# MLP gates of a decoder layer: the side pass's subtractions moved to VectorE at three fixed places, signs stored in the base's tile, VectorE and TensorE in written order

## The chip, the cores and the metric

One core of a Trainium2 chip runs the whole kernel in one launch. The time is the device time of that core in microseconds (us). The core's engines run side by side, each in its own instruction order: TensorE (PE, with PEld for its weight loads), VectorE (DVE), ScalarE (ACT), GpSimd (POOL) and SyncE (SP, which here only issues DMAs). They meet through semaphores. TensorE writes its products to eight banks of PSUM; everything else lies in SBUF.

## The reference

A decoder layer in float32 on 2 x 512 tokens of width 1024: a Mamba-2 block with a gated MLP behind it, a product with a quantized context, and a gated FFN whose weights are rebuilt from a base and the signs of a difference. What matters here are the MLP and what the FFN needs of its weights:

```python
h2 = rmsnorm(h, ln2_w)
mlp = silu(h2 @ gate_w.T) * (h2 @ up_w.T) @ down_w.T      # INTER = 3584
...
def _binary_diff_weight(w, base):
    d = w - base
    coeff = jnp.mean(jnp.abs(d))
    return base + coeff * jnp.sign(d)
W1 = _binary_diff_weight(w1, mean_w1)
W2 = _binary_diff_weight(w2, mean_w2)
W3 = _binary_diff_weight(w3, mean_w3)
```

The mean of |d| runs over a whole weight matrix, so the kernel must have passed over all of w1, w2 and w3 before the FFN begins. It does this pass beside the MLP: it stores the signs in bf16 and sums the absolute values.

## The kernel before

**Stages.** The MLP ("m") and the FFN ("f") use the same two functions: `gates` makes silu(gate) * up and stores it with the differences of the down weights, `down` multiplies them. `gates` takes the 3584 columns in 14 groups of 256 (NG, GW). A group is one 2 x 2 block product by Winograd's form of Strassen's scheme with seven block products; two of the seven pairs are split once more by `second_level`. So a group has, on TensorE, `second_level` "m" (products 1 and 2 of the outer scheme, L779, tiles mm{i}a to d), `second_level` "n" (6 and 7, tiles mn{i}a to d) and three calls of `one` (products 5, 4 and 3, L857, tiles m{i}c and m{i}d). Groups 0 and 1 have plain products in place of "m" (`first_two`, L328, tile ma).

**Banks.** "m" and the calls of `one` use four of the eight banks (X), "n" the other four (Y); the next group has them the other way round. In `second_level` bank b is written by product 6, read by VectorE's add u2, and written again by product 7; bank c is written by product 5, read by the add c22, and written on by product 3. Bank a is copied to p1 by ScalarE (L786) ahead of u2. Inside one, the written order on TensorE is a1, b6, c5, d4, b7, a2, c3.

**VectorE's work of a group** (helpers `add` L187 and `sub` L190): five adds that empty the banks in each `second_level`; the add to O12 (mo, 128x1024); two adds of 128x1024 that end in `turn` (L888); two adds each for the banks of products 5 and 4 (the last add of product 4 gives block 21) and two for product 3 (`finished`); `left`, the block differences of the next group's gate and up weights (four each, tiles mg{i}s and mu{i}s, and four more for "n"); `outer_left`, four more for "m" (tile my and others); `down_blocks`, four for the down weights; four products of silu(gate) and up (L925, tile mh); `hidden_blocks`, four differences of mh. `left`, `outer_left` and `down_blocks` may not be issued ahead of `turn`. Apart from that the scheduler orders VectorE and TensorE: it puts what is ready first, earlier lines ahead of later ones. In group 1 there are four more of 128x1024 (`second_level_right`, B12).

**The deferred part.** In the MLP a group's last steps wait in the list `late` and are written inside the next group: `finished` (the two adds for product 3, Silu, the product of slot 3) behind the copy of bank a, `put` (`hidden_blocks` and the store of mh) behind the "m" `second_level`.

**The side pass** (`Diffs`, only in the MLP, 34 steps, three a group, the last in group 11). A step takes one group of w1, w3 or w2 (128x2048 float32, 1 MB, and as much for the base). GpSimd loads both by its own DMA queue (tiles sw with two buffers and smean_w with one, L1137), subtracts (L1152) and stores the signs (L1142); ScalarE computes Sign into a bf16 tile sg (L1161) and Abs with a running sum (L1162). ScalarE's order in this stage is the written one (`on_act`, a chain of `issue_after` edges, which fix an order on one engine without a wait); GpSimd's is too (`on_pool`). `Diffs.step` is called in the "n" `second_level` (`between`), after the three first products of silu and up, and in `finished`.

**Queues.** SP loads gate and up weights (L172), the down weights (L1117), and stores the differences of the down weights (L1118) and mh (L942). `down` reads both stores back when the gates are done.

Of the kernel before, what the change touches and what calls it, by code (L numbers as in the profile page):

```python
# [10 lines left out]
F32 = mybir.dt.float32  # L11
BF16 = mybir.dt.bfloat16
AF = mybir.ActivationFunctionType
ALU = mybir.AluOpType
# [24 lines left out]
def decoder(ctx, tc, a, out):  # L39
# [146 lines left out]
    def add(out_, x, y):  # L186
        nc.vector.tensor_tensor(out_, x, y, ALU.add)  # L187

    def sub(out_, x, y):
        nc.vector.tensor_tensor(out_, x, y, ALU.subtract)  # L190
# [89 lines left out]
    def hidden_blocks(h):  # L280

        a11, a12, a22, a21, s2, s3, s4 = (h[:, i, :] for i in range(7))
        sub(s3, a11, a21)
        add(a21, a21, a22)
        sub(s2, a21, a11)
        sub(s4, a12, s2)
# [8 lines left out]
    act_last = []  # L295

    def on_act(fn):
        with tc.issue_after(act_last[0]) if act_last and act_last[0] else nullcontext():
            ins = fn().ins
        if act_last:  # L300
            act_last[:] = [ins]
# [17 lines left out]
    def first_two(name, act, pl, i, gw, uw, banks):  # L319
# [4 lines left out]
        def step(p, x, w):  # L324
            if not p:
                ps.append(bank(banks[x], f"{name}a{x}_{i}"))
            for k in range(4):
                nc.tensor.matmul(  # L328
                    ps[x], w[:, 4 * p + k, :P], act[0][:, 4 * p + k, :],
                    start=not p and k == 0, stop=k == 3, skip_group_check=p > 0,  # L330
                )
# [440 lines left out]
    def second_level(name, banks, p1, A, B, O, copied=lambda: None, between=lambda: None):  # L772
# [12 lines left out]
        mm("a", 1)  # L785
        on_act(lambda: nc.scalar.copy(p1, ps["a"]))  # L786
        copied()
        mm("b", 6)
        add(u2, p1, ps["b"])
        mm("c", 5)  # L790
        mm("d", 4)
        mm("b", 7, True)
        add(u3, p1, ps["b"])
        add(c22, u3, ps["c"])
        mm("a", 2, True)
        on_act(lambda: nc.scalar.copy(c11, ps["a"]))
        between()
        add(u3, u3, ps["d"])
        mm("c", 3, True)
        add(u2, u2, ps["c"])  # L800

    def gates(name, act, acts, g, pl, weights, down_weight, begun, ex, side):
# [4 lines left out]
        act_last[:] = [None] if side else []  # L807
# [4 lines left out]
        with g:  # L812
# [6 lines left out]
            def outer_left(i, gw, uw):  # L819

                gv, uv = (w[:, :, :P].rearrange("p (q k) c -> p q k c", q=2) for w in (gw, uw))
                y = pl["y12"].tile([P, 2 if side else 4, 2, 2, P], F32, tag="y", name=f"{name}y12_{i}")
                if side:
                    s4 = pl["y12_"].tile(None, F32, "y", f"{name}y12_{i}s4")
                    return second_level_left(gv, uv, uv[:, :, :2], y[:, 0], y[:, 1], s4)
                return second_level_left(gv, uv, *(y[:, j] for j in range(4)))

            def left(i, gw, uw):

                s23, A = [], []  # L830
                for x, w in (("g", gw), ("u", uw)):
                    a11, a12, a21, a22 = (w[:, k : k + 4, c : c + P] for c in (0, P) for k in (0, 4))
                    two = pl["s23"].tile([P, 2, 4, P], F32, tag=x, name=f"{name}{x}{i}s")
                    four = pl["s4"].tile([P, 4, P], F32, tag=x, name=f"{name}{x}{i}s4")
# [3 lines left out]
                    sub(four, a12, two[:, 0])  # L838
# [3 lines left out]
                return A, second_level_left(s23[0], s23[1], s23[1][:, :, :2], *(y[:, j] for j in range(3)))  # L842

# [3 lines left out]
            for i in range(NG):  # L847
# [3 lines left out]
                def one(x, p, onto=False, into={}):  # L851
# [3 lines left out]
                    for j in range(2):  # L855
                        for k in range(4):
                            nc.tensor.matmul(  # L857
                                into[x][j], A[j][p][:, k, :], B[p][:, k, :],
                                start=not onto and k == 0, stop=k == 3, skip_group_check=onto,
                            )  # L860
# [4 lines left out]
                elif i < 2:  # L865
                    O12, steps = first_two(name, act, pl, i, *coming[0], X)
                    for n, step in enumerate(steps):
                        if n == 2:
                            for part in late:
                                part()  # L870
                        step()
                else:
                    O12 = pl["o12" if "o12" in pl else "o1"].tile([P, 2, 2, L], F32, tag="o", name=f"{name}o12_{i}")
                    p1 = pl["px"].tile([P, 2, Q], F32, tag="p", name=f"{name}p12_{i}")
                    first, then = late or (lambda: None, lambda: None)
                    second_level(f"{name}m{i}", X, p1, A12, B12, O12, first)
                    then()
                    add(O12[:, 1], O12[:, 0], O12[:, 1])
# [7 lines left out]
                second_level(f"{name}n{i}", Y, p1, A67, B67, O67, between=side or (lambda: None))  # L886
                add(O67[:, 0], O12[:, 0], O67[:, 0])
                turn = nc.vector.tensor_tensor(O67[:, 1], O67[:, 0], O67[:, 1], ALU.add).ins  # L888
# [558 lines left out]
```

## Time and profile before

| what | value |
|---|---|
| median of 3 runs | 2444.61 us (2444.18 to 2454.88) |
| the profiled execution | 2444.3 us, its span 2442.5 us |
| granted TensorE clock, mean of the span | 0.990 |
| MLP gates, groups 0 and 1: mn0a to mm2a | 502.9 to 574.8 us |
| MLP gates, start of mm2a, mm3a, mm4a, mm5a, mm6a, mm7a | 574.8, 624.3, 673.5, 721.6, 769.9, 819.1 us |
| start of mm8a, mm9a, mm10a, mm11a, mm12a, mm13a | 868.2, 916.3, 965.6, 1014.8, 1063.0, 1108.1 us |
| FFN gates, start of fm3a, fm4a, fm5a and of fm13a | 1647.1, 1692.0, 1736.8 and 2095.7 us |
| GpSimd's 34 subtractions (L1152) | 4.50 us at the least, 4.52 median, 11.92 at the most |
| landing of a load of 1 MB by GpSimd's queue, median and longest | w 5.5 and 14.5 us, base 5.8 and 10.0 us |
| landing of a store of mh, median and longest | 13.6 and 16.6 us |

The page gives each engine's busy time as a share of the span; a window is the same for a stretch, with the granted clock, the share of time in which the 16 DMA engines were busy, and what they moved. A line of waits names who waited for whom: microseconds in total, times, longest. A line of the timeline is an instruction or a run of like ones: start, duration, engine, line, operation, what it writes and reads, and in brackets how long the engine had been idle and who released it. The start of a group is the first MATMUL of its product mm a or fm a in the list of the tile's instructions. A MATMUL row of a run of eight ends somewhat after the next run starts, since they are pipelined; the spacing of the starts is the time that counts: 1.73 us for a second-level product, 6.87 for a call of `one`.

### The profile page before, as it was taken

The page shows a single profiled execution, that of the slowest core. Times are in us where ns is not written, and L with a number is a line of the kernel's source. Part 1 is how long each engine was busy: PE and PEld are TensorE (multiplying, and loading weights), DVE is VectorE, ACT ScalarE, POOL GpSimd, SP SyncE. Part 2 cuts the span into 40 slices and gives each one's busy share as a digit, 9 for nine tenths or more (in the row PEclk, how much of TensorE's full clock was granted, in tenths as well). Part 3 has the DMA queues.
Part 4 walks back from the last instruction along what each step waited for, and adds up shares of the span by engine and source line. Part 5 has one row for each costly group of instructions (what it writes and reads, how often), then busy time and mean ns, then how long its engine had stood idle before and what let it go on. Part 6 is the DMA issues. An engine that isn't in the chain of part 4 may idle for free.

```text
span 2442.5 us, 23439 instructions
## 1 busy us (share of the span) xinstructions
PE 2364.9 (97%) x8732; PEld 1604.9 (66%) x8740; DVE 1685.3 (69%) x2410; ACT 607.9 (25%) x776; POOL 397.6 (16%) x280
## 2 busy tenths in 40 slices
PE   7999999999999999999999999999999999999999
PEld 5445444456566656666888775667667667688888
DVE  4757777577888888776555656686775776665554
ACT  3355460333333333211000234232132221100000
POOL 1124211254344434400000010000000000000000
PEclk8999999999999999999999999999999999999999
DMA  4353541658778778847765480676667577686652
GB/s 149 120 204 122 174 164 69 194 203 331 296 301 321 288 294 303 313 172 274 221 187 166 122 266 35 165 197 190 193 186 209 157 201 204 223 257 193 201 168 65
DMA packets 183634, 494.50 MB, mean 202 GB/s; under 512 B 21472, under 2 KB 125920, under 8 KB 152544
## 3 DMA queue, kind: packets, MB, share of 16 engines
q1 hardware_dynamic: 155360, 334.65, 39.5%
q0 software_dynamic: 23552, 149.96, 21.2%
q10 hardware_dynamic: 4608, 8.39, 0.9%
q8 instruction: 69, 1.13, 0.2%
q14 instruction: 45, 0.37, 0.1%
HBM read 349.26 MB, written 145.75 MB: 203 GB/s over the span
## 4 chain that ended last, share of the span: by engine, by line
PE 74%; DVE 15%; issue 4%; DMA 3%; SPq 2%; ACT 1%; POOL 1%; DVEq 0%; POOLq 0%; ACTq 0%
PE op L673 3%; DVE mh L925 2%; DVE mpl L187 2%; SPq L978 2%; DVE acc L543 1%; DVE down L190 1%; DVE mo L187 1%; PE ma L328 1%; PE dps L449 1%; DVE mpl L190 1%; PE fa L328 1%; PE m0c L857 1%; PE f1c L857 1%; PE f0c L857 1%; PE f11c L857 1%
## 5 line engine op out<-in xcount | busy, mean ns | idle before, releaser
L1152 POOL TENSOR_TENSOR sw<-sw,smean_w 128x2048 f32<-128x2048 f32 x34 | 191.3, 5626 | 28.8 <-DMA smean_w<-in_mean_w 28.5
L1348 POOL DMA_DIRECT2D fw<-in_mean_w x42 | 36.5, 868 | 527.2 <-ACT fw L1347 472.9
L1347 ACT ACTIVATE fw<-fpl,coeff 128x2048 f32<-128x2048 bf16 x38 | 76.2, 2004 | 92.7 <-DMA fpl<-sign 20.1
L385 POOL TENSOR_TENSOR raw<-raw,base 128x1024 f32<-128x1024 f32 x16 | 42.4, 2649 | 207.3 <-DMA base<-in_mean_w 61.1
L1161 ACT ACTIVATE sg<-sw 128x2048 bf16<-128x2048 f32 x34 | 64.8, 1906 | 34.7 <-POOL sw L1152 34.7
L923 ACT ACTIVATE fo<-fo 128x512 f32<-128x512 f32 x56 | 35.0, 626 | 137.4 <-DVE fo L187 137.2
L1162 ACT ACTIVATE sw<-sw 128x2048 f32<-128x2048 f32 x34 | 65.0, 1911 | 1.1
L673 PE MATMUL op<-wout,mz 128*128 128x512 f32 x128 | 56.6, 592 | 0.0
L925 DVE TENSOR_TENSOR mh<-mpl 128x512 f32<-128x512 f32 x28 | 51.5, 1840 | 5.6 <-ACT mpl L923 4.4
L1142 POOL DMA_DIRECT2D sign<-sg x34 | 18.3, 539 | 226.6 <-ACT sg L1161 216.9
L91 POOL TENSOR_TENSOR q_r<-q_e,mhalf 128x1 f32<-128x1 f32 x8 | 7.0, 877 | 255.5 <-DVE q_e L87 242.4
L923 ACT ACTIVATE mpl<-mpl 128x512 f32<-128x512 f32 x28 | 17.7, 631 | 115.5 <-DVE mpl L187 115.4
L673 PEld LDWEIGHTS op<-wout,mz 128*128 128x128 f32 x128 | 24.0, 191 | 28.1 <-issue 27.7
L925 DVE TENSOR_TENSOR fh<-fo 128x512 f32<-128x512 f32 x56 | 36.3, 684 | 1.6
L187 DVE TENSOR_TENSOR mo<-mo 128x1024 f32<-128x1024 f32 x12 | 36.3, 3028 | 1.3
L190 DVE TENSOR_TENSOR down<-down 128x512 f32<-128x512 f32 x56 | 37.1, 678 | 0.0
L923 ACT ACTIVATE mo<-mo 128x512 f32<-128x512 f32 x28 | 17.5, 624 | 73.8 <-DVE mo L187 73.8
L187 DVE TENSOR_TENSOR hid<-hid,op 128x512 f32<-128x512 f32 x24 | 15.9, 683 | 24.0 <-PE op L673 24.0
L619 POOL TENSOR_TENSOR mz<-mz,ys 128x512 f32<-128x512 f32 x16 | 20.7, 1294 | 65.9 <-DVE ys L616 44.8
L328 PE MATMUL fa<-x3T,fw 128*128 128x512 f32 x64 | 28.7, 595 | 2.1 <-ACT fo L332 2.1
L118 PE MATMUL h1T<-ident,h 128*128 128x128 f32 x64 | 13.4, 361 | 17.6 <-ACT h L440 10.8
L190 DVE TENSOR_TENSOR fh<-fh 128x512 f32<-128x512 f32 x42 | 29.0, 690 | 1.0
(2263 smaller groups left out, 6017.4 us busy)
## 6 DMA issues: line engine op xcount, KB each, us to landing
fw<-in_mean_w POOLq DMA_DIRECT2D x42, 1024.0 KB, 13.6
sw<-in_w POOLq DMA_DIRECT2D x34, 1024.0 KB, 5.5
smean_w<-in_mean_w POOLq DMA_DIRECT2D x34, 1024.0 KB, 5.8
mwd<-down SPq DMA_DIRECT2D x14, 1792.0 KB, 7.4
mhd<-mh SPq DMA_DIRECT2D x13, 1792.0 KB, 13.6
fhd<-fh SPq DMA_DIRECT2D x13, 1792.0 KB, 8.1
fpl<-sign SPq DMA_DIRECT2D x38, 512.0 KB, 8.9
sign<-sg POOLq DMA_DIRECT2D x34, 512.0 KB, 3.0
```

The lines of the kernel that those rows point to most:

```text
L187: nc.vector.tensor_tensor(out_, x, y, ALU.add)
L190: nc.vector.tensor_tensor(out_, x, y, ALU.subtract)
L328: nc.tensor.matmul(ps[x], w[:, 4 * p + k, :P], act[0][:, 4 * p + k, :], start=not p and k == 0, stop=k == 3, skip_group_check=p > 0,)
L673: nc.tensor.matmul(ps, A[p][:, k, t * P : t * P + P], B[p][:, k, :], start=(k == 0), stop=(k == 3))
L857: nc.tensor.matmul(into[x][j], A[j][p][:, k, :], B[p][:, k, :], start=not onto and k == 0, stop=k == 3, skip_group_check=onto,)
L923: on_act(lambda: nc.scalar.activation(o[:, 0], o[:, 0], AF.Silu))
L925: nc.vector.tensor_tensor(h[:, slot, :], o[:, 0], o[:, 1], ALU.mult)
L978: nc.sync.dma_start(tl[:, c, :], dr[c][:, slot, col * Q : col * Q + Q])
L1152: self.on_pool(lambda: nc.gpsimd.tensor_tensor(w, w, v, ALU.subtract))
L1161: on_act(lambda: nc.scalar.activation(sg, w, AF.Sign))
L1162: on_act(lambda: nc.scalar.activation(w, w, AF.Abs, accum_out=sums[:, j, 2 * i : 2 * i + 1]))
L1347: nc.scalar.activation(dst, src, AF.Identity, scale=coeff[:, j : j + 1])
```

## The change

- GpSimd subtracts no more; it issues the loads and stores of the side pass. VectorE does the subtraction, in `step`, through the function that is handed to it.
- Both tiles of a step have two buffers, and two steps are loaded ahead. The signs go into the first half of the base's tile as bf16, and the store reads them there; the tile sg is gone. The load of step n + 2 is issued behind step n.
- The three places are: in "n" behind the add u2 (`summed67`), with the add to O12 moved there from the end of "m"; behind the add that ends block 21 (`blocks21`); and in the next group's "m" behind its add u2 (`last_product`), ahead of the product of slot 3.
- `on_dve` and `on_pe` chain instructions in their written order in the MLP: all of `second_level`, `finished`, `hidden_blocks`, the adds that end in `turn`, and every product on TensorE. `left`, `outer_left`, `down_blocks`, the first three products of silu and up and the adds for products 5 and 4 are not in the chain.
- The fourth difference of the gate weights, which product 3 needs, is taken from `left` and done in the next group's "m" (`take_fourths`). Its tile has one buffer, p1 has one place in place of two, and `outer_left` has fixed places for two of its differences.

The diff, cut to its core:

```diff
+    def ordered(last_, fn):
+        with tc.issue_after(last_[0]) if last_ and last_[0] else nullcontext():
+            ins = fn().ins
+        if last_:
+            last_[:] = [ins]
+        return ins
+    def on_dve(fn):
+        return ordered(dve_last, fn)
+    def on_pe(fn):
+        with tc.issue_after(pe_last[0]) if pe_last and pe_last[0] else nullcontext():
+            fn()
+        if pe_last:
+            pe_last[:] = [last_on(mybir.EngineType.PE)]
...
-    def second_level(name, banks, p1, A, B, O, copied=lambda: None, between=lambda: None):
+    def second_level(name, banks, p1, A, B, O, copied=lambda: None, summed=lambda: None):
...
+        on_pe(lambda: mm("a", 1))
         on_act(lambda: nc.scalar.copy(p1, ps["a"]))
         copied()
+        on_pe(lambda: mm("b", 6))
+        on_dve(lambda: add(u2, p1, ps["b"]))
+        summed()
+        on_pe(lambda: mm("c", 5))
+        on_pe(lambda: mm("d", 4))
+        on_pe(lambda: mm("b", 7, True))
+        on_dve(lambda: add(u3, p1, ps["b"]))
+        on_dve(lambda: add(c22, u3, ps["c"]))
+        on_pe(lambda: mm("a", 2, True))
         on_act(lambda: nc.scalar.copy(c11, ps["a"]))
-        between()
...
                     sub(two[:, 0], a21, a11)
-                    sub(four, a12, two[:, 0])
+                    fourths.append(lambda four=four, a12=a12, two=two: sub(four, a12, two[:, 0]))
+                    if not side or not i or x == "u":
+                        fourths.pop()()
...
+            def take_fourths():
+                while fourths:
+                    on_dve(fourths.pop(0))
...
-                    first, then = late or (lambda: None, lambda: None)
-                    second_level(f"{name}m{i}", X, p1, A12, B12, O12, first)
-                    then()
-                    add(O12[:, 1], O12[:, 0], O12[:, 1])
+                    first, second, third = late or [lambda: None] * 3
+                    def summed():
+                        second()
+                        take_fourths()
+                    second_level(f"{name}m{i}", X, p1, A12, B12, O12, first, summed)
+                    third()
+                    if not side:
+                        add(O12[:, 1], O12[:, 0], O12[:, 1])
...
+                def summed67(i=i, O12=O12):
+                    if side:
+                        side(on_dve)
+                        if i > 1:
+                            on_dve(lambda: add(O12[:, 1], O12[:, 0], O12[:, 1]))
+                second_level(f"{name}n{i}", Y, p1, A67, B67, O67, summed=summed67)
...
-                    add(O67[:, 1, j], O67[:, 1, j], d[j])
+                    blocks21 = add(O67[:, 1, j], O67[:, 1, j], d[j]).ins
...
+                def finished(c=c, O67=O67):
                     for j in range(2):
-                        add(O67[:, 0, j], O67[:, 0, j], c[j])
-                    product(3, O67[:, 0])
+                        on_dve(lambda: add(O67[:, 0, j], O67[:, 0, j], c[j]))
+                    on_act(lambda: nc.scalar.activation(O67[:, 0, 0], O67[:, 0, 0], AF.Silu))
+                def last_product(O67=O67, h=h, more=side and not last):
                     if more:
-                        side()
+                        side(on_dve)
+                    on_dve(lambda: nc.vector.tensor_tensor(h[:, 3, :], O67[:, 0, 0], O67[:, 0, 1], ALU.mult))
...
                 if side and not last:
-                    side()
-                    late.extend([finished, put])
+                    with tc.issue_after(blocks21):
+                        side(lambda fn: fn())
+                    late.extend([finished, last_product, put])
...
-            w, v = self.raw[n]
-            self.on_pool(lambda: nc.gpsimd.tensor_tensor(w, w, v, ALU.subtract))
-            self.load(n + 1, 1)
...
+        def load(self, n):
             if n < len(self.todo):
                 i, j = self.todo[n]
+                self.raw[n] = []
+                for tag, x in zip(("raw", "base"), FFN[j]):
+                    tl = pl["raw"].tile([P, KC * GW], F32, tag=tag, name=f"s{x}{i}")
+                    self.raw[n].append(tl)
+                    ordered(self.pool_last, lambda: nc.gpsimd.dma_start(tl, flat(a[x][i])))
+        def step(self, dve):
             if self.n == len(self.todo):
                 return
             i, j = self.todo[self.n]
+            w, b = self.raw.pop(self.n)
+            dve(lambda: sub(w, w, b))
+            sg = b.bitcast(BF16)[:, : KC * GW]
             on_act(lambda: nc.scalar.activation(sg, w, AF.Sign))
             on_act(lambda: nc.scalar.activation(w, w, AF.Abs, accum_out=sums[:, j, 2 * i : 2 * i + 1]))
+            ordered(self.pool_last, lambda: nc.gpsimd.dma_start(signs[j][i], sg))
+            self.load(self.n + 2)
             self.n += 1
```

## The prediction

> **What bounds the kernel now.** I read the engines' totals, then one group of the MLP's gates (m) beside one of the FFN's (f), then TensorE's (PE's) waits, then the order of events around one wait.
>
> ```profile
> PE 2364.9 (97%) x8732; PEld 1604.9 (66%) x8740; DVE 1685.3 (69%) x2410; ACT 607.9 (25%) x776; POOL 397.6 (16%) x280
> ...
> 769.90:819.10 49.20, 46.77 (x162) 31.38 (x161) 40.50 (x48) 16.29 (x18) 20.69 (x12) 0.97 0.78 299
> ...
> 1647.10:1692.00 44.90, 44.90 (x162) 30.27 (x161) 31.35 (x47) 10.70 (x12) 2.61 (x3) 1.00 0.66 186
> ```
>
> TensorE sets the time, so only what makes it wait, or slows its clock, can be won. The two window lines (columns: length; busy PE, weight loads, DVE, ACT, POOL; granted clock; DMA share; GB/s) are one group of each stage, and the same 162 matmul records. The f group has no wait. The m group has 2.43 us of it, a clock of 0.97, and a VectorE (DVE) that is busy 9.15 us longer for practically the same instructions. From the starts of the groups, f takes 44.86 us each (fm3a 1647.1 to fm13a 2095.7, ten groups) and m 48.82 (mm2a 574.8 to mm12a 1063.0, ten groups): 39.6 us above f's pace.
>
> ```profile
> PE mm2b L779 <- DVE mo L187: 2.7, 1, 2.7
> PE mm9b L779 <- DVE mo L187: 2.5, 1, 2.5
> ...
> 752.69 5.49 DVE L190 TENSOR_TENSOR mg6s<-gate_w 128x512 f32<-128x512 f32 x1
> 753.11 4.51 POOL L1152 TENSOR_TENSOR sw<-sw,smean_w 128x2048 f32<-128x2048 f32 x1
> ...
> 771.44 6.75 POOL L1152 TENSOR_TENSOR sw<-sw,smean_w 128x2048 f32<-128x2048 f32 x1
> 775.12 3.63 DVE L925 TENSOR_TENSOR mh<-mpl 128x512 f32<-128x512 f32 x1
> 778.67 0.67 DVE L187 TENSOR_TENSOR mo<-mpl,mm6b 128x512 f32<-128x512 f32 x1
> 779.39 2.70 PE L779 MATMUL mm6b<-mex,my 128*128 128x256 f32 x8 [2.43 <-DVE mo L187]
> 781.89 2.91 PE L779 MATMUL mm6a<-h2T,gate_w 128*128 128x256 f32 x8
> 784.64 1.89 PE L779 MATMUL mm6c<-h2T,mpl 128*128 128x256 f32 x8
> ```
>
> Each of groups 2 to 11 waits at the same place: product 7 into bank b, until VectorE's add u2 has read the bank. The reason is above it: a VectorE instruction of 0.68 us takes 5.49 or 3.63 and ends with GpSimd's (POOL's) subtraction, 757.62 and 778.19. Before it VectorE had 27 instructions from 752.69; 27 x 0.60 plus the 4.81 too much gives 773.7, where the two `finished` adds do stand. Then 2.95 more is lost in mh, u2 ends at 779.34, and PE, due at 776.8, starts at 779.39. After the wait 2.70 and 2.91 stand where 1.89 is usual: the clock is the rest of the 4.3 us (49.2 - 44.86 - 2.43 = 1.9; 0.8 in the groups of 48.1).
>
> The Trainium skill ("TensorE: Matmul & The Clock Gate", section "What's actually happening") has the array fall to half its clock only after an idle window of about 3.4 us. By that rule a wait of 2.43 us would be harmless to the clock and its removal would return ten times 2.43, not 39.6 us; the rows 2.70 and 2.91 say otherwise, and I go by them.
>
> **The change, part by part.** t counts from the first MATMUL of a group's product mm a.
>
> *GpSimd's 34 subtractions go*, and with them the 9.15 us a group by which VectorE is stretched. GpSimd's DMA issues stay; beside one (770.89) VectorE's mh at 770.73 took 0.68, so they hold nothing up.
>
> *VectorE gets three subtractions of 128x2048 a group.* The trace has none of that size. From 512 to 1024 columns the time goes from 0.68 to 1.225, so 2048 would end after 2.31 and free the engine after some 2.25; four instructions of 512 at their spacing would be 2.41, twice 1024 at 1.14 (489.75 to 490.88) 2.28. I take 2.25: 6.75 a group against 9.15 lost now. Load: 31.35 + 6.75 = 38.1 of 44.9 us, so it fits, and what counts is where they stand.
>
> The Trainium skill ("Perfetto Trace Analysis", section "Optimizing Scalar/DVE Operations") warns that, since the two engines share an SBUF read port, moving work between them might not help. By that rule this part would be worth nothing and the time would stay 2444; the rows give VectorE 2.4 us a group back.
>
> ```profile
> 1673.61 1.22 DVE L888 TENSOR_TENSOR fo<-fo 128x1024 f32<-128x1024 f32 x1
> 1690.99 0.68 DVE L187 TENSOR_TENSOR fo<-fo,f3c 128x512 f32<-128x512 f32 x1
> ...
> 1656.66 0.69 DVE L187 TENSOR_TENSOR fo<-fo,fm3c 128x512 f32<-128x512 f32 x1
> ...
> 766.56 1.89 ACT L1161 ACTIVATE sg<-sw 128x2048 bf16<-128x2048 f32 x1
> 768.49 1.91 ACT L1162 ACTIVATE sw<-sw 128x2048 f32<-128x2048 f32 x1
> 770.30 0.19 ACT L1162 ACTIVATION_READ_ACCUMULATOR sw<-sw 128x1 f32 x1
> 771.83 0.58 ACT L786 COPY mpl<-mm6a 128x512 f32<-128x512 f32 x1 [1.33 <-PE mm6a L779]
> ```
>
> *Place 1, after the blocks of 21* (`blocks21`). In f VectorE is free of `turn` (L888) at 1674.75 and runs 27 instructions to 1690.99 (0.6015 each); fm4a starts at 1692.0. Afterwards there are 26 (the fourth difference of the gates moves away) and the subtraction: 1674.75 + 15.64 + 2.25 = 1692.64, t = 0.64, if it stands last, as it is written last. Then ScalarE (ACT), in its fixed order: Sign from 0.74, the accumulator read 3.93 later (766.56 to 770.49), then only the copy p1, 4.69 to 5.27. The add u2 needs p1 and bank b; b is ready at 3.6, so p1 decides and u2 starts at 5.31. It has read the bank at 6.0, in time for product 7 at 6.9.
>
> *Place 2, the first second_level.* Behind u2: the subtraction 5.91, the product of slot 3 8.16, the fourth difference 8.76, u3 9.36, c22 10.08 to 10.77. In f c22 ends at 1657.35, t = 10.25, and product 3 starts on it. So a new wait of 0.5 us a group, at bank c instead of b. The 0.38 us waits of today (mm5c) are followed by matmuls of 1.99 where 1.89 is usual, so I charge no clock for it. Bounds: subtraction 1 earlier by two instructions of 0.6 takes the wait away (0); behind the two `finished` adds it is 1.7, with the clock's 0.8 to 1.9 on top.
>
> *Place 3, the second second_level.* u2 at 16.3 (after hidden_blocks, which move ahead of it by order), subtraction to 19.15, the moved O12 add to 20.35; u3 is due at 21.4. Cover 1.0 us, cost nothing; beyond that each us is PE's.
>
> *Loads and stores.* Signs into the base's place chain store and reload: place 1's Sign ends at 2.6, its store lands 3.0 later, the base's load is issued at about 6.5 and needed two steps on, at 16.9: 10.4 us. The queue behind it on POOL holds only place 2's store, due later.
>
> ```profile
> sw<-in_w POOLq DMA_DIRECT2D x34, 1024.0 KB, 5.5
> smean_w<-in_mean_w POOLq DMA_DIRECT2D x34, 1024.0 KB, 5.8
> sign<-sg POOLq DMA_DIRECT2D x34, 512.0 KB, 3.0
> ```
>
> Median 5.8, longest 10.0 us for the base (14.5 for one w): hidden. The traffic of 299 GB/s packed into 45.4 us would be 324, where slices of 331 exist. SP's queue keeps its order.
>
> *Group 2* has four further 128x1024 differences (B12, 1.14 each) in VectorE's stretch: t = 0.64 + 4.6 = 5.2, p1 9.8, u2 to 10.6, a wait of 3.7 at bank b and 1.9 for the clock: 50.5 against 49.5 today, +1.0.
>
> *TensorE's fixed order.* After mn0 today 12 matmul records of group 1 (5.15 us) run ahead of m0c, which then waits 4.23 (until 524.57) behind a stretched mg1s. In the written order m0c comes first and waits from 515.0 for mg1s and two adds, 518.42 + 0.6 + 1.27 = 520.3; the 5.15 follow: 525.4, +0.9. Everywhere else the order in the trace is the written one: nothing.
>
> **The sum.** Groups 3 to 11: 438.7 (624.3 to 1063.0) to 9 x 45.36 = 408.2, -30.5. Groups 2: +1.0; 0 and 1: +0.9; group 12 (45.1): -0.2. Together -28.8. The profiled execution took 2444.3 (span 2442.5 and 1.8 around it; median of the runs 2444.61), so 2415.5. Nothing later eats this up: the down product behind runs on the same loads, shifted.
>
> **Rivals.**
> *A, no new wait.* Subtraction 1 stands two or more instructions earlier. For: VectorE's order is filled by readiness (mh stands between the down differences). Against: it is written last. Groups 2 to 11 at 44.86 save 39.6; with +0.9 and group 2's cost anywhere from none to the 5.6 above: 2405 to 2411.
> *B, the wait only moves.* ScalarE's copy p1 comes after Sign and Abs in a fixed order; if subtraction 1 falls behind the two adds, 1.7 + 0.8 to 1.9 a group: 47.4 to 48.5, nine groups 426 to 436, 2434 to 2444. For: 26 instructions and one of 2.25 overrun mm a's start. Against: its place in the text is ahead of those adds.
> *C, slower: a late load at place 3.* VectorE is in order, so the subtraction's wait for its base holds u3 and c22, and PE at bank c. A landing longer than 10.4 + 1.0 us becomes a wait, with the clock's 1.9 on it; a group has 48.8 - 45.4 = 3.4 us to give, so the gain is gone at a landing of 12.9, and 14.3 makes the kernel slower by over 0.5%. At 16.6, the longest landing of mhd, the wait is 5.2 + 1.9: nine groups of 52.5, 472, 2479. For: 0.78 of the DMA engines busy already. Against: the medians.
> The change not doing what it says: POOL has no other two-operand work in these groups, so its hold on VectorE must go.
>
> **How the numbers follow.** Forecast, the wait at bank c between 0.1 and 1.2 (2411 to 2424): 0.50, 2415. A: 0.25. B: 0.16, half of it above 2432. C: 0.05, and 0.04 for what I don't see. A measurement of this kernel tells 0.5% (12 us) from no change, so faster is below 2432: 0.50 + 0.25 + 0.08 + 0.02 = 0.85; same 0.09; slower 0.06. Range 2402 to 2436: A's lower end with smaller costs in groups 0 to 2, and the near part of B.
>
> **What would show it.** mh, the first mg difference and mo<-mo 128x1024 at 0.68, 0.68 and 1.23; new 128x2048 rows of about 2.3 on DVE; PE's wait at mm-b gone from groups 3 to 11 and one of about 0.5 at mm-c; group starts 45.4 apart; granted clock 1.00. Wrong if DVE waits for smean_w, if mm-b waits stay near 2.4, or if f's groups change too.

## The result and the profile after

The changed kernel takes 2407.43 us (median of 4 runs, 2404.69 to 2410.29), the kernel before 2446.86 in the same comparison (2444.18 to 2454.88): a ratio of 0.9834, 95% interval 0.9807 to 0.9861. It is faster by 1.7%, inside the forecast range and 7.6 us below the forecast time. The profiled execution took 2404.69 us with a span of 2402.9, against 2444.3 and 2442.5.

First the totals of the engines, from the page of the kernel after:

```profile
PE 2349.6 (98%) x8740; PEld 1596.1 (66%) x8740; DVE 1649.6 (69%) x2444; ACT 606.7 (25%) x776; POOL 205.0 (9%) x246
```

POOL fell from 397.6 to 205.0 us. VectorE has 34 instructions more, of 2.29 us each, and is still busy 35.7 us less: the stretching that is gone was more than the subtractions cost it. The windows of one MLP group and of one FFN group (columns as before) show the same in a group:

```profile
754.20:799.50 45.30, 45.15 (x162) 30.27 (x161) 37.76 (x51) 16.14 (x17) 4.80 (x9) 1.00 0.86 325
```

```profile
1607.60:1652.50 44.90, 44.90 (x162) 30.25 (x161) 31.35 (x47) 10.70 (x12) 2.61 (x3) 1.00 0.68 192
```

VectorE is 6.41 us busier than in f, three subtractions and no stretch; the clock is back at 1.00. The starts of ten groups (mm2a 573.3, mm12a 1025.6) are 45.23 apart, where they were 48.82 and f's are 44.86. The waits of TensorE and VectorE in the stage:

```profile
PE m0c L884 <- DVE mo L187: 4.6, 1, 4.6
PE ma L343 <- ACT mo L349: 3.0, 1, 3.0
PE fa L343 <- ACT fo L349: 2.1, 1, 2.1
PE mo6b L1038 <- DVE mw6e L187: 0.8, 1, 0.8
...
DVE sw L190 <- DMA smean_w<-in_mean_w: 1.6, 1, 1.6
```

The ten waits at bank b are gone. What is left stands in groups 0 and 1 (m0c, ma), behind the gates (fa, mo6b), and in one late base load. The small wait at bank c that comes below has no row in the list; it is read from the starts in the timeline. Now the order around the old wait, group 6, from the timeline:

```profile
752.66 2.30 DVE L190 TENSOR_TENSOR sw<-sw,smean_w 128x2048 f32<-128x2048 f32 x1
754.24 1.89 PE L796 MATMUL mm6a<-h2T,gate_w 128*128 128x256 f32 x8
754.86 1.29 DVE L187 TENSOR_TENSOR mpl<-mpl,m5c 128x512 f32<-128x512 f32 x2
754.99 1.91 ACT L1194 ACTIVATE smean_w<-sw 128x2048 bf16<-128x2048 f32 x1 [8.73 <-DVE sw L190]
...
756.93 1.91 ACT L1195 ACTIVATE sw<-sw 128x2048 f32<-128x2048 f32 x1
...
758.84 0.57 ACT L803 COPY mpl<-mm6a 128x512 f32<-128x512 f32 x1
...
759.44 0.69 DVE L187 TENSOR_TENSOR mo<-mpl,mm6b 128x512 f32<-128x512 f32 x1 [3.29 <-ACT mpl L803]
760.04 2.29 DVE L190 TENSOR_TENSOR sw<-sw,smean_w 128x2048 f32<-128x2048 f32 x1
761.14 1.89 PE L796 MATMUL mm6b<-mex,mpl 128*128 128x256 f32 x8
761.55 0.53 POOL L1185 DMA_DIRECT2D smean_w<-in_mean_w  x1 [1.69 <-DMA sign<-smean_w]
762.24 0.69 DVE L978 TENSOR_TENSOR mh<-mpl 128x512 f32<-128x512 f32 x1
...
763.45 0.68 DVE L187 TENSOR_TENSOR mo<-mpl,mm6b 128x512 f32<-128x512 f32 x1
764.16 0.69 DVE L187 TENSOR_TENSOR mo<-mo,mm6c 128x512 f32<-128x512 f32 x1
...
764.90 1.35 PE L796 MATMUL mm6c<-h2T,mpl 128*128 128x256 f32 x5
...
771.06 2.29 DVE L190 TENSOR_TENSOR sw<-sw,smean_w 128x2048 f32<-128x2048 f32 x1
```

Read it with t = 0 at 754.24. The first subtraction stands ahead of the two `finished` adds and the second behind u2 (759.44). VectorE idles 3.29 us for p1, which ScalarE copies at 758.84, after Sign and Abs. Product 7 into bank b starts on time at 761.14. Product 3 into bank c starts at 764.90 instead of 764.60 (1.73 behind the product ahead of it), and the next one, at 766.74, follows after 1.84 instead of f's 1.77: this 0.37 us is the whole difference between 45.23 and f's pace.

The landing of the side pass's transfers (columns: count, KB, median us from issue to landing), which were 5.5, 5.8 and 3.0:

```profile
sw<-in_w POOLq DMA_DIRECT2D x34, 1024.0 KB, 7.7
smean_w<-in_mean_w POOLq DMA_DIRECT2D x34, 1024.0 KB, 7.8
sign<-smean_w POOLq DMA_DIRECT2D x34, 512.0 KB, 6.3
```

Where the 39.6 us of the span come from, by the starts of tiles in both profiles:

| stretch | before | after | difference | forecast |
|---|---|---|---|---|
| up to mn0a | 502.9 | 498.1 | -4.8 | 0 |
| groups 0 and 1: mn0a to mm2a | 71.9 | 75.2 | +3.3 | +0.9 |
| group 2 | 49.5 | 45.2 | -4.3 | +1.0 |
| groups 3 to 11 | 438.7 | 407.1 | -31.6 | -30.5 |
| mm12a to mo1a | 89.9 | 89.7 | -0.2 | -0.2 |
| mo1a to fm3a | 494.2 | 492.3 | -1.9 | 0 |
| fm3a to the end | 795.4 | 795.3 | -0.1 | 0 |

### The profile page after: what moved, and what is told of

Same layout as the page of the kernel before. It is cut to its first block, busy times and chain, and to the rows that moved or that the text cites. A ratio compares the mean times of both kernels' runs of the same rounds, so it can differ in the third digit from the quotient of the medians.

```text
span 2402.9 us, 23501 instructions
## 1 busy us (share of the span) xinstructions
PE 2349.6 (98%) x8740; PEld 1596.1 (66%) x8740; DVE 1649.6 (69%) x2444; ACT 606.7 (25%) x776; POOL 205.0 (9%) x246
## 4 chain that ended last, share of the span: by engine, by line
PE 76%; DVE 16%; issue 3%; ACT 2%; DMA 2%; SPq 1%; POOL 1%; DVEq 0%; POOLq 0%; ACTq 0%
PE op L690 3%; DVE sw L190 2%; DVE mpl L187 2%; DVE acc L560 1%; DVE mo L187 1%; DVE down L190 1%; DVE mpl L190 1%; ACT smean_w L1194 1%; PE dps L466 1%; PE fa L343 1%; PE ma L343 1%; PE xa L1296 1%; SPq L1027 1%; DVE mh L968 1%; PE f1c L884 1%
## 5 line engine op out<-in xcount | busy, mean ns | idle before, releaser
L1194 ACT ACTIVATE smean_w<-sw 128x2048 bf16<-128x2048 f32 x34 | 65.0, 1911 | 175.2 <-DVE sw L190 175.2
L1376 ACT ACTIVATE fw<-fpl,coeff 128x2048 f32<-128x2048 bf16 x38 | 76.1, 2004 | 90.5 <-DMA fpl<-sign 17.4
L190 DVE TENSOR_TENSOR sw<-sw,smean_w 128x2048 f32<-128x2048 f32 x34 | 77.8, 2289 | 1.6 <-DMA smean_w<-in_mean_w 1.6
L966 ACT ACTIVATE fo<-fo 128x512 f32<-128x512 f32 x42 | 26.2, 625 | 90.8 <-DVE fo L187 90.7
L1196 POOL DMA_DIRECT2D sign<-smean_w x34 | 18.3, 538 | 292.1 <-ACT smean_w L1194 291.8
L690 PEld LDWEIGHTS op<-wout,mz 128*128 128x128 f32 x128 | 23.9, 190 | 27.7 <-issue 27.3
L187 DVE TENSOR_TENSOR fo<-fo 128x1024 f32<-128x1024 f32 x26 | 31.8, 1225 | 1.7
L966 ACT ACTIVATE mpl<-mpl 128x512 f32<-128x512 f32 x14 | 8.8, 630 | 89.1 <-DVE mpl L187 89.1
L118 PE MATMUL h1T<-ident,h 128*128 128x128 f32 x64 | 13.8, 368 | 17.9 <-ACT h L457 11.1
L190 DVE TENSOR_TENSOR mh<-mh 128x512 f32<-128x512 f32 x42 | 29.0, 690 | 0.9
L1185 POOL DMA_DIRECT2D smean_w<-in_mean_w x34 | 18.2, 534 | 127.3 <-DMA sign<-smean_w 32.8
L1296 PE MATMUL xa<-c,c1T 128*128 128x512 bf16 x128 | 28.8, 379 | 0.0
L968 DVE TENSOR_TENSOR fh<-fo 128x512 f32<-128x512 f32 x42 | 26.9, 696 | 0.2
## 6 DMA issues: line engine op xcount, KB each, us to landing
fw<-in_mean_w POOLq DMA_DIRECT2D x42, 1024.0 KB, 13.6
```

The lines of the kernel that those rows point to most:

```text
L187: return nc.vector.tensor_tensor(out_, x, y, ALU.add)
L190: return nc.vector.tensor_tensor(out_, x, y, ALU.subtract)
L690: nc.tensor.matmul(ps, A[p][:, k, t * P : t * P + P], B[p][:, k, :], start=(k == 0), stop=(k == 3))
L966: on_act(lambda: nc.scalar.activation(o[:, 0], o[:, 0], AF.Silu))
L968: nc.vector.tensor_tensor(h[:, slot, :], o[:, 0], o[:, 1], ALU.mult)
L1194: on_act(lambda: nc.scalar.activation(sg, w, AF.Sign))
```

## The experiments

Two theories share the reading of the trace before. **L, the hold:** GpSimd's subtraction stretches whatever VectorE runs beside it; what counts is that another engine does it. **O, the order:** a stretched or a long VectorE instruction costs only where it stands ahead of an instruction that empties a bank; what counts is what the written order puts ahead of u2, u3 and c22. "Ten groups" is the time from mm2a to mm12a, "0 and 1" that from mn0a to mm2a, both in the profiled execution.

| kernel | median us | ratio to before, 95% | ten groups | 0 and 1 |
|---|---|---|---|---|
| before | 2445.1 to 2450.8 in the comparisons | 1 | 488.2 | 71.9 |
| after | 2407.43 | 0.9834 (0.9807 to 0.9861) | 452.3 | 75.2 |
| e5 before, no subtraction | 2400.48 | 0.9820 (0.9790 to 0.9850) | 448.5 | 66.1 |
| e6 after, no subtraction | 2403.30 | 0.9831 (0.9811 to 0.9851) | 448.5 | 72.0 |
| e1 after, GpSimd subtracts | 2415.32 | 0.9879 (0.9861 to 0.9897) | 462.1 | 73.1 |
| e3 after, both chains out | 2441.48 | 0.9973 (0.9956 to 0.9989) | 486.8 | 73.0 |
| e12 e3, GpSimd subtracts | 2446.60 | 0.9983 (0.9964 to 1.0002) | 494.6 | 74.4 |
| e4 after, TensorE's chain out | 2404.48 | 0.9829 (0.9813 to 0.9845) | 454.9 | 70.8 |
| e2 before, VectorE subtracts | 2497.16 | 1.0208 (1.0191 to 1.0225) | 536.3 | 67.3 |
| e7 before, slot 3 behind u2 | 2439.16 | 0.9973 (0.9958 to 0.9987) | 478.4 | 72.8 |
| e8 Sign and Abs behind p1 | 2426.26 | 0.9919 (0.9887 to 0.9952) | 466.2 | 78.6 |
| e10 only Abs behind p1 | 2403.80 | 0.9819 (0.9792 to 0.9846) | 448.6 | 77.5 |
| e11 e10, TensorE's chain from group 1 | 2408.12 | 0.9836 (0.9806 to 0.9867) | 448.6 | 76.1 |
| e13 e10, groups 0 and 1 rearranged | 2398.72 | 0.9798 (0.9782 to 0.9815) | 448.6 | 74.2 |

**e5 and e6: what is there to win.** The subtraction is taken out of each kernel and the rest stays. The signs and sums are then those of w, so these two do not compute the layer; they only show what the subtraction costs.

```diff
-            self.on_pool(lambda: nc.gpsimd.tensor_tensor(w, w, v, ALU.subtract))
...
-            dve(lambda: sub(w, w, b))
```

> The kernel before with the 34 subtractions left out: nobody subtracts, Sign and Abs work on w itself, so the signs and sums are those of w; loads, stores and orders as before. It asks what the hold of GpSimd's subtraction on VectorE costs in the order of before. Theory L as I predicted it: all waits at bank b of mm go, groups take 44.9 to 45.2, 2400 to 2410. Theory O in its strong form (the order is at fault even without the hold): waits at bank b of over 1 us remain, 2420 or more.

> The kernel after with the 34 subtractions left out in the same way. It asks what VectorE's own subtractions cost. My ledger: the wait of 0.37 at bank c goes, groups from 45.23 to 44.86 to 44.9, ten groups 3.5 us, groups 0 and 1 little changed: 2400 to 2405. Rival: the subtractions are hidden wholly and the 0.37 is something else: no change, 2405 to 2409.

The ten groups take 448.5 us in both, which is f's pace (448.6). A window of e5's group 6:

```profile
747.80:792.65 44.85, 44.85 (x162) 30.27 (x161) 31.36 (x47) 16.18 (x17) 4.80 (x9) 1.00 0.89 333
```

TensorE is never idle, VectorE needs 31.36 us as in f, and all the DMAs run (0.89, 333 GB/s). So in the order of before the subtraction on GpSimd cost 39.7 us in ten groups and nothing else cost anything; after the change it costs 3.8. This is what L forecast for e5: in the old order the hold alone makes the loss. O in its strong form, an order at fault even without the hold, falls.

**e1: the new order with the old engine.**

```diff
-            dve(lambda: sub(w, w, b))
+            ordered(self.pool_last, lambda: nc.gpsimd.tensor_tensor(w, w, b, ALU.subtract))
```

> The kernel after, with its order, its places for Sign and Abs and its loads two steps ahead, but GpSimd does the 34 subtractions again. Theory L (GpSimd's subtraction holds VectorE's two-operand instructions for its whole length, and that made the waits): VectorE's 128x512 rows next to a subtraction are again 3 to 5.5 us, VectorE is busy about 40 us a group, groups take 47 to 50 us, and the time is 2430 to 2450. Theory O (the fixed order and the places brought the gain, whoever subtracts): groups stay at 45.2 and the time within 2400 to 2412. Theory B (the loads two steps ahead and the second base buffer brought it): as O.

Measured 2415.32, far below L's range and just above O's: most of the gain is there though GpSimd subtracts. The timeline of e1 in group 6:

```profile
763.42 4.56 POOL L1192 TENSOR_TENSOR sw<-sw,smean_w 128x2048 f32<-128x2048 f32 x1
...
764.69 0.69 DVE L187 TENSOR_TENSOR mo<-mpl,mm6b 128x512 f32<-128x512 f32 x1
765.29 3.24 DVE L978 TENSOR_TENSOR mh<-mpl 128x512 f32<-128x512 f32 x1
...
770.50 1.99 PE L796 MATMUL mm6c<-h2T,mpl 128*128 128x256 f32 x8 [0.50 <-DVE mo L187]
```

The hold is unchanged: mh takes 3.24 us. But u2 now stands ahead of it, so bank b is free in time, and what it costs here is 0.50 at bank c. The list of e1's waits has ten in the ten groups, of 0.4 to 1.9 us and 9.3 in all, eight of them in "n". u2 itself ran in 0.69 during the same subtraction; it reads a bank. So L alone falls for the new order.

**e3 and e12: the three places without the order.** The chains of VectorE and TensorE are left out, with VectorE (e3) and with GpSimd (e12) subtracting.

```diff
-        act_last[:] = dve_last[:] = pe_last[:] = [None] if side else []
+        act_last[:] = [None] if side else []
```

> The kernel after without the written order on VectorE and on TensorE (ScalarE's stays); subtractions by VectorE, called at the same three places. Theory L: within 10 us of the kernel after (2397 to 2417), groups at 44.9 to 46. Theory O: the order is what holds the group together, groups 47 or more and 2425 to 2450.

> GpSimd subtracts, the loads go two steps ahead and the calls stand at the three places, but neither VectorE nor TensorE has the written order. It asks whether the small loss of GpSimd's subtraction in the order of after (ten groups 462.1) came from the order on VectorE or from loads and places. Order: the ten groups take 478 to 490 us, 2430 to 2445. Loads and places: 460 to 466, 2412 to 2420.

Without the order nearly all of the gain is gone with either engine; e12 is even slower than O forecast. In e12 the waits at bank b are back; the timeline of its group 6 shows the same picture as before the change:

```profile
771.75 4.53 POOL L1192 TENSOR_TENSOR sw<-sw,smean_w 128x2048 f32<-128x2048 f32 x1
771.99 4.85 DVE L190 TENSOR_TENSOR mg6s<-gate_w,mg6s 128x512 f32<-128x512 f32 x1
...
778.14 0.68 DVE L187 TENSOR_TENSOR mo<-mpl,mm6b 128x512 f32<-128x512 f32 x1
...
778.88 1.99 PE L796 MATMUL mm6b<-mex,mpl 128*128 128x256 f32 x8 [3.05 <-DVE mo L187]
```

In e3 nothing is stretched. There the scheduler puts the third subtraction ahead of "n"'s u2, and its base is not yet there:

```profile
781.39 0.53 POOL L1185 DMA_DIRECT2D smean_w<-in_mean_w  x1 [1.68 <-DVE mh L190]
...
793.04 2.29 DVE L190 TENSOR_TENSOR sw<-sw,smean_w 128x2048 f32<-128x2048 f32 x1 [5.46 <-DMA smean_w<-in_mean_w]
...
796.38 0.68 DVE L187 TENSOR_TENSOR mpl<-mpl,mn6b 128x512 f32<-128x512 f32 x1
...
797.12 2.00 PE L796 MATMUL mn6b<-mpl,mpl 128*128 128x256 f32 x8 [3.37 <-DVE mpl L187]
```

VectorE stands 5.46 us for a DMA, with u2 queued behind, and TensorE waits 3.37 at bank b of "n". In all of e3 VectorE waits 48.3 us for the base, 11 times. So the order saves different things: from GpSimd's hold it keeps a bank's add from standing behind a stretched instruction, and with VectorE it keeps the add from standing behind a subtraction that waits for its load. How much of e3's loss an earlier load alone would save was not tried. The four corners of engine and order, in us over ten groups of one execution each (no subtraction: 448.5):

| who subtracts | places alone | places and written order | worth of the order |
|---|---|---|---|
| GpSimd | 494.6 (e12) | 462.1 (e1) | 32.5 |
| VectorE | 486.8 (e3) | 452.3 (after) | 34.5 |
| worth of VectorE | 7.8 | 9.8 | |

By the ratios of the runs in the first table the order is worth 1.0% with GpSimd and 1.4% with VectorE (25 and 34 us), and VectorE 0.45% (11 us) with the order. Without the order the two engines can't be told apart: the intervals of e12 and e3 overlap, and most of the 7.8 is clock (27.3 us of e12's ten groups ran at half clock, 13.7 of e3's).

**e4: which chain.** TensorE's chain alone is left out.

```diff
-        act_last[:] = dve_last[:] = pe_last[:] = [None] if side else []
+        act_last[:] = dve_last[:] = [None] if side else []
```

> The kernel after without the written order on TensorE alone. My reading of groups 0 and 1 (75.2 us against 71.9 before; the product c3 of group 0 in front of group 1's plain products costs a wait of 4.57 with nothing to fill it, and the plain products then wait 2.98 for ScalarE): with the order free the plain products run ahead again, mn0a to mm2a takes 68 to 72 us, groups 2 to 11 stay at 45.2, and the time falls by 3 to 7 us to 2400 to 2404. Rival: TensorE's order matters in the steady groups too, then those change by more than 0.2 us each.

The ten groups lose 2.6 us and groups 0 and 1 gain 4.4; the median, 2404.48, can't be told from the change's. So the order that is worth 25 to 34 us must in the main be VectorE's; a run without that chain alone was not made.

**e2: the engine without places or order.** In the kernel before, only the engine of the subtraction is changed.

```diff
-            self.on_pool(lambda: nc.gpsimd.tensor_tensor(w, w, v, ALU.subtract))
+            nc.vector.tensor_tensor(w, w, v, ALU.subtract)
```

> The kernel before, with its order and its single base buffer, but VectorE does the 34 subtractions where the scheduler puts them. Theory L: no VectorE instruction of 128x512 is stretched beyond 0.7 us, the waits at bank b of mm shrink to under 1 us, groups take 45 to 46.5 and the time is 2402 to 2420, unless VectorE now waits for a load. Theory O: without the places the subtraction stands where it holds u2 or c22 up, groups take 47 to 50, 2430 to 2455. Theory B: the single base buffer makes VectorE wait for the base's DMA, as GpSimd did (28.5 us in all), 2430 to 2450.

A miss: 2497.16, 2.1% slower than before. Its waits:

```profile
DVE sw L1152 <- DMA smean_w<-in_mean_w: 84.9, 22, 5.9
...
PE mm7c L779 <- DVE mo L187: 4.9, 1, 4.9
```

The base has one buffer there, so its load starts only when the step before has been subtracted. On GpSimd that wait held nobody up; VectorE passes it on to TensorE. How much of the loss is the single buffer and how much the missing order this run can't tell.

**e7: one part of the order in the kernel before.** The product of slot 3 (mh) is issued behind u2.

```diff
-                    product(3, O67[:, 0])
+                    on_act(lambda: nc.scalar.activation(O67[:, 0, 0], O67[:, 0, 0], AF.Silu))
...
+                    with tc.issue_after(u2 or turn):
+                        nc.vector.tensor_tensor(h[:, 3, :], O67[:, 0, 0], O67[:, 0, 1], ALU.mult)
```

> The kernel before with one change of order: the product of slot 3 (mh, 3.63 us when GpSimd holds it up) is issued behind the add u2 of mm instead of ahead of it; GpSimd still subtracts. Theory O, as the run with GpSimd's subtraction in the order of after suggests (what the hold stretches must only not stand ahead of u2): the waits at bank b of mm fall from 2.4 to under 0.7, groups take 45 to 46.8, 2405 to 2428. Theory L (the hold itself must go): some other instruction ahead of a bank's add is held, groups stay above 48, 2435 to 2447.

2439.16 is a gain of 0.3%, less than O forecast (2405 to 2428) and in L's range. Group 6 of e7 in the timeline:

```profile
768.23 0.69 DVE L187 TENSOR_TENSOR mo<-mpl,mm6b 128x512 f32<-128x512 f32 x1
768.82 3.24 DVE L935 TENSOR_TENSOR mh<-mpl 128x512 f32<-128x512 f32 x1
...
773.54 1.42 DVE L190 TENSOR_TENSOR mh<-mh 128x512 f32<-128x512 f32 x2
774.88 0.68 DVE L187 TENSOR_TENSOR mo<-mpl,mm6b 128x512 f32<-128x512 f32 x1
...
776.34 1.99 PE L779 MATMUL mm6c<-h2T,mpl 128*128 128x256 f32 x8 [1.53 <-DVE mo L187]
```

Bank b is free early, but behind the stretched mh come `hidden_blocks` (to 774.9) and only then u3; the wait moved to bank c, 2.6 us in eight of the ten groups. One place is not enough; e1, in which u3 and c22 are ordered too, waits at most 0.9 at this bank. The ten groups gain 9.8 us although the waits are as long as before, since the clock was lost after one of them instead of six: 3.4 us of them ran at half clock instead of 20.5 (last section). So this gain is not shown to be the order's.

**e8 and e10: the 0.37 us at bank c.** p1 stands behind Sign and Abs on ScalarE. e8 puts both behind the copy p1 and Silu, e10 only Abs, so that the sign store is not later.

```diff
-                        side(lambda fn: fn())
-                    late.extend([finished, last_product, put])
+                        rest = side(lambda fn: fn(), True)
+                    def finished_then(finished=finished, rest=rest):
+                        finished()
+                        rest()
+                    late.extend([finished_then, last_product, put])
```

> The kernel after, but ScalarE does Sign and Abs of place 1 behind the copy p1 and the Silu of the next group instead of ahead of them. My ledger says the copy p1 waits 4 us for them, which sets u2, c22 and the wait of 0.37 at bank c, and in group 1 the 2.98 before ma: groups 44.9, group 1 shorter by 2 to 3, 2399 to 2404. Rival: ScalarE's order does not decide, the 0.37 stays.

> The kernel after, but at place 1 ScalarE does Sign ahead of the copy p1 of the next group and only Abs behind it and the Silu; the store of the signs keeps its place, the load of w comes about 1 us later. If the copy p1 alone sets the wait at bank c, and the loss of the run with both moved came from the later store and base load (VectorE waited 32 us for smean_w there): no waits at bank c, VectorE waits for smean_w under 5 us in all, groups 44.9, the ten groups 452.3 to 449, 2400 to 2405. Rival: the later load of w is late in its turn, groups 45.5 or more and 2408 or more.

e8 missed, 2426.26. It does take the wait at bank c away, but the sign store and the base load behind it are issued later:

```profile
DVE sw L190 <- DMA smean_w<-in_mean_w: 32.0, 11, 7.2
...
PE mn8c L796 <- DVE mpl L187: 2.7, 1, 2.7
PE mn5c L796 <- DVE mpl L187: 2.4, 1, 2.4
```

In group 6 the base load is issued at t = 11.1 where the change has 7.3, and the third subtraction waits for it. That is the forecast's rival C, made by 3.8 us of lateness. e10, which moves Abs alone, has no wait in the ten groups: 448.6, f's pace. The kernel as a whole (2403.80) is not told apart from the change: groups 0 and 1 lengthen by 2.3.

**e11 and e13: groups 0 and 1.** e11 adds to e10 that TensorE's chain begins in group 1. e13 keeps the chain and, in group 0, writes product 3 behind group 1's first two plain products, with the Sign and Abs of that step behind the copies of those products.

```diff
+                if i == 1 and side:
+                    pe_last[:] = [last_on(mybir.EngineType.PE)]
```

```diff
+                            first_c3()
...
-                one("c", 3, True)
+                if i == 0 and side:
+                    def first_c3(A=A, c=c):
...
+                else:
+                    one("c", 3, True)
...
+            if n != 1:
+                signed()
```

> As e10_abs_after_p1, and TensorE's written order begins only with group 1, so that group 1's plain products may run ahead of c3 of group 0. Expected: groups 0 and 1 from 75.2 to 70 to 72, the ten groups 449, 2395 to 2401, faster than both kernels. Rival: the free order costs waits in group 1 at mn1c again (3.2 in the run without the written order), 2400 to 2405.

> As e10_abs_after_p1, and in group 0 alone: the product c3 is written behind the first two plain products of group 1, and ScalarE does both Sign and Abs of place 1 behind those products' copies and the Silu. My reading of groups 0 and 1 (77.5 us in e10: m0c waits 4.6 with nothing to fill it, ma waits for a copy that stands behind Sign, mn1c waits 2.5) gives: no wait at m0c, ma under 1, groups 0 and 1 at 66 to 70, the rest as e10, 2392 to 2398. Rival: the later sign store of that one step makes VectorE wait for smean_w at place 3 of group 1, mn1c waits 3 to 6, and groups 0 and 1 stay at 72 to 76, 2398 to 2404.

e11 missed (2408.12): the wait of 4.6 at m0c became one of 7.5 at ma for the copy behind Sign. e13 takes 2398.72 us (five runs, 2396.90 to 2399.07), just above what was expected and where its rival put it: the third subtraction of group 1 waits 4.2 us for its base, mn1c waits 3.6, and groups 0 and 1 take 74.2. Its waits of TensorE in the stage:

```profile
PE mn1c L796 <- DVE mpl L187: 3.6, 1, 3.6
PE ma L343 <- ACT mo L349: 2.9, 1, 2.9
```

m0c's wait is gone, two others stay. All five runs lie below all four of the change's; the two were measured on different chips, and their ratios to before, 0.9798 (0.9782 to 0.9815) and 0.9834 (0.9807 to 0.9861), just overlap. It is the fastest of the kernels that compute everything.

## Why the prediction was right, and where not

**What bounds the kernel: right.** That TensorE is held by waits that GpSimd's subtraction causes, and that f's pace is the floor, is shown by e5: 448.5 us without it.

**The places: right to 0.2 us.** Forecast and measured t in group 6: end of subtraction 1 0.64 and 0.62; u2 5.31 and 5.20; subtraction 2 5.91 and 5.80; u3 9.36 and 9.21; c22 from 10.08 and from 9.92; a new wait at bank c of 0.5 and 0.37. The price of a 128x2048 subtraction, 2.25 from spacing, measured 2.20. Rivals A and B are both refuted by these rows: a wait is there, and it is not at bank b. e10 shows that the copy p1 behind Sign and Abs makes the 0.37, as the step said: Abs behind it takes the wait away.

**The number: in part luck.** The new wait lies in the band that was given for it, 0.1 to 1.2 us, but 2407.43 does not lie in the time given with that band (2411 to 2424); it lies in that of rival A, whose condition did not come. Group 2 was 5.3 us better than forecast, groups 0 and 1 were 2.4 worse, and 6.7 came from stretches that the forecast put at nothing.

**Why it works: only in part as put.** That the hold makes the loss in the old order is right (e5). But the part "GpSimd's 34 subtractions go, and with them the 9.15 us" is credited with too much: the forecast had the order in its ledger, yet treated the engine as the cure. With the order and GpSimd (e1) the hold costs 13.6 us over the floor instead of 46.1 (e12), and VectorE without the order (e3) loses nearly all of the gain, with 48.3 us of waits for the base. The order is worth 25 to 34 us, the change of engine 8 to 11 with the order.

The Trainium skill ("Perfetto Trace Analysis", section "Optimizing Scalar/DVE Operations") warns that moving work between GpSimd and VectorE might not help, since they share a read port. The forecast went by the rows and against it. Measured, the move is worth 8 to 11 us where places and buffers fit it, and e2, the bare move, lost 51. The warning held for the bare move, though what shows there is a wait for the base's DMA and not the port.

**The clock: the rule used was too simple.** The forecast put down 1.9 us of clock to a wait of 2.43, and 0.8 in the groups of 48.1. In those groups no clock was lost at all (see the last section). Their rest is the second wait, at bank c: 0.38 in the list of waits, and with the 0.1 to 0.2 us that the starts show around each wait beyond the list, 0.8. The sum was not hurt, since it was made against the measured group.

**Group 2: the step that failed.** The forecast had four B12 differences of 1.14 in VectorE's stretch ahead of mm2a and a wait of 3.7: +1.0. They run some 30 us before mm2a, in both kernels; after:

```profile
489.31 1.23 DVE L190 TENSOR_TENSOR mex<-h2T 128x1024 f32<-128x1024 f32 x1
...
540.33 1.23 DVE L190 TENSOR_TENSOR mex<-h2T 128x1024 f32<-128x1024 f32 x1
541.59 1.23 DVE L190 TENSOR_TENSOR mex<-h2T,mex 128x1024 f32<-128x1024 f32 x1
```

Group 2 is like the others, 45.2: -4.3. The trace before has the same rows at 492.62, 546.14 and 547.40.

**Groups 0 and 1: mis-sized.** The wait at m0c came as forecast (4.57, to 514.94; the forecast's sum makes it 5.3). Missed was the next: ma waits 2.98 at 533.62 for ScalarE's copy of its bank, which stands behind the Sign and Abs of a step. So +3.3 instead of +0.9. e6 without any subtraction takes 72.0 there and e5 66.1, so the subtraction is not what costs most here; e4, without TensorE's chain, gets 4.4 back. The term rested on TensorE's order alone and left out the copy behind ScalarE's work.

**Loads: hidden, by less than put.** The load was issued at t = 7.3 rather than 6.5 and needed at 16.8; the store ahead of it landed in 6.3 us and the load in 7.8, where the forecast took 3.0 and 5.8 over from the kernel before. Slack at the median was 1.7 us, not 4.6 (10.4 less 5.8). One wait of 1.6 us came of it. e8 and e3 show how near C was: issued four microseconds later, or needed three earlier, the load is waited for.

**Before and behind the gates: not in the forecast.** -4.8 up to mn0a and -1.9 from mo1a to fm3a, 6.7 of the 10.8 us by which the profiled gain exceeded the forecast. mn0a starts between 496.1 and 504.0 in the other kernels that differ only in the gates (513.4 in e2), and mo1a to fm3a takes 490.1 to 499.0. The only subtraction in either stretch is the first one of the kernel before (487.42), and TensorE has no gap between it and mn0a. In good part the differences go with the clock: in the kernel before 6.8 us between 340 and 481 us and 3.4 us between mo1a and fm3a ran at half clock, in the kernel after none. Over all 14 profiled executions mo1a to fm3a takes 490.1 to 492.3 us where no clock was lost, 493.9 to 495.8 where 3.4 us ran at half clock, and 494.3 to 499.0 where more did. Why the clock fell there in some kernels was not tried and stays open.

## What to carry to other kernels

What a long instruction on a shared engine costs depends on where it stands: the same hold cost 46.1 us in one order and 13.6 in another (e12, e1). Before moving such an instruction to another engine, look at what is queued behind it that empties a bank, and fix that order first. When the work moves to an engine that others wait for, its loads must be early enough that this engine never stands for a DMA, so give them a second buffer with the move. After such an edit, read every in-order engine that got work (here ScalarE's p1 and ma copies), not only the one that was relieved.

## What the runs showed of the hardware

**A wait's cost in clock depends on where it falls in windows of 3.41 us.** The first two rows below are the kernel before, group 5, with the same wait of 2.42 to 2.43 us that in its group 6 was followed by 2.70 and 2.91; the others are e7, two equal waits.

```profile
731.12 1.99 PE L779 MATMUL mm5b<-mex,my 128*128 128x256 f32 x8 [2.42 <-DVE mo L187]
732.96 1.89 PE L779 MATMUL mm5a<-h2T,gate_w 128*128 128x256 f32 x8
```

```profile
824.04 3.68 PE L779 MATMUL mm7c<-h2T,mpl 128*128 128x256 f32 x8 [2.62 <-DVE mo L187]
...
873.43 1.99 PE L779 MATMUL mm8c<-h2T,mpl 128*128 128x256 f32 x8 [2.62 <-DVE mo L187]
```

Over the waits of 1 us and more in the ten groups of before, e1, e2, e3, e7, e8 and e12, slowed matmuls followed 1 of 19 waits of 1.0 to 2.3 us, 12 of 24 of 2.4 to 2.8, and 19 of 22 of 2.8 to 4.9. The Trainium skill ("TensorE: Matmul & The Clock Gate", section "What's actually happening") says that the window of activity runs freely, about 3.4 us long; that fits equal waits with unequal ends. Its other statement, that a whole idle window must pass, does not fit the 13 slowed cases below 2.8 us.

The granted clock in these traces shows what sets them apart. Within the gates the stretches at half clock last 3.41 or 6.83 us, and in each trace they begin whole multiples of 3.41 us apart, so they mark windows. In group 6 of the kernel before the clock is at half from 780.53 to 783.94; the window ahead runs from 777.12, and 2.27 us of it are wait (776.96 to 779.39), a share of 0.67. Taken so for every wait, by the window it fills most, the share separates them: of the 65 waits, none of the 32 with at most 0.55 of a window slowed the clock, and 32 of the 33 with 0.57 or more did (the other had 0.59). The wait of group 5 above fills 0.52 at most, the two of e7 0.77 and 0.43. The shortest wait that slowed the clock was 1.93 us long, the longest that did not 3.37.

**The hold spares what reads a bank.** In e1 u2 took 0.69 us in the midst of a GpSimd subtraction, while the next instruction, with both inputs in SBUF, took 3.24 and ended 0.6 us after it.

**A store's landing doubled, and why is open.** The median store of 512 KB landed after 6.3 us instead of 3.0, the load of 1 MB after 7.8 instead of 5.8, with the DMA engines' share over the ten groups at 0.85 instead of 0.79. The store's new source (the base's tile instead of sg) is not the reason: e2 and e5 store from sg, and there it landed after 6.3 and 6.2 us. Nor is the mean share alone: it is 0.70 in e2, and 0.81 in e7, where the store landed after 3.2.
